# First LSTM steps as seven half-block products, two units in three sets, with the cell product on GpSimd

## The chip, the cores and the metric

The kernel runs on one core of one Trainium2 chip. The metric is device time in microseconds (us), the median of several runs. The engines are TensorE (PE: matmuls; PEld is its weight load), VectorE (DVE), ScalarE (ACT), GpSimd (POOL) and SyncE (SP, whose queue issues most DMAs). Matmul results land in PSUM, eight banks of 128 x 512 float32; everything else works from SBUF. Everything is float32.

## The reference, cut to what matters

Four layers are applied in turn to x [128 batches, 64 nodes, 256 features], each as x = x + layer(relu(layernorm(x))). The change touches the first one alone: two graph convolutions give h [128, 64, 256], and then four LSTMs, one for each window length p, run over windows of h and write each window's last hidden state back into it:

```python
def step(carry, x_t):
    h, c = carry
    g = x_t @ Wih.T + h @ Whh.T + bias
    i, f, gg, o = jnp.split(g, 4, axis=-1)
    c = sigmoid(f) * c + sigmoid(i) * tanh(gg)
    h = sigmoid(o) * tanh(c)
    return ((h, c), None)          # zero initial state
...
for p in range(1, MAX_SKIP + 1):   # MAX_SKIP = 4
    nw = Tv // p
    wins = h[:, :nw * p, :].reshape(Bv * nw, p, Hd)
    last = _lstm_last(Wih[p - 1], Whh[p - 1], bih[p - 1], bhh[p - 1], wins)
    idx = jnp.arange(nw) * p + (p - 1)
    h = h.at[:, idx, :].set(last.reshape(Bv, nw, Hd))
```

In a window's first step h and c are zero: the f gate plays no part, and the three gates i, g and o come from x alone (256 features in, 3 x 256 out). Later steps need four gates from x and h (512 in, 4 x 256 out).

## The kernel before, in words

h lies in four tiles `hs`, [128 features of a half c, c, node, 32 batches]. The LSTM works in units: one window length p, two of the tiles (two blocks of batches, `blk`), and nk windows (8, 8, 7, 8 for p = 1 to 4), so a block has n = nk x 32 columns, 256 or 224. The loop at L565 runs over p, then over pairs of units (8, 4, 3 and 2 pairs, 17 in all), then over the steps t, and in each step over the two units. `unit` (L429) makes a unit's closures and `step` (L519) issues one step.

A step with t = 0 uses `first_gates` (L452): for each gate and each half m of its outputs, a bank is filled by four matmuls (two halves c of the features, two blocks), 24 in a step and 48 for a pair, each of 128 x 128 weights by 128 x n columns (L459). ACT applies the gate function from PSUM (`act`, L444 to L446). DVE multiplies i by g into the cell (L529), ACT takes its tanh (L538), and DVE multiplies with o into the hidden state (L540), or, in the last step of a window, into `hs` (L547).

A later step uses `next_gates` (L466). It splits weights and moving data into 2 x 2 blocks, and computes each pair of gates by seven block products in place of eight (Winograd's form of Strassen's algorithm). `sums` (L190) makes four sums of weight blocks, once per p, in `blocks_of` (L551), which also negates one block (L561); `moving_blocks` (L497) makes four differences of the moving blocks in each step (L504 to L509). `sevens` (L208) pairs them up and `seven` (L153) issues them: products 1, 5, 6 and 7 into four banks, two copies out of PSUM on ACT (L162, L163), two additions on DVE (L165, L166); then, in `finish`, one addition on POOL (L169), products 2, 4 and 3 on top of three of the banks, two more DVE additions (L174, L177), and the gate functions through `end`. Each product is four matmuls here (two gates, two chunks, L471). `finish` is called at once.

Written order is a priority only. The tile framework fills each engine's queue by a plan of its own: an instruction is placed when its inputs and its tile's buffer are planned to be ready, the earliest written first. On the chip each engine then works its queue strictly in that order. The buffers that can hold an instruction back are eight PSUM banks, and for tags `gates` three, `p15`, `diff` and `state` two each, and five weight tiles `w` in pool `lw`. A sixth weight tile (`weight_tile`, L63) gets the attention weights (L572), whose DMA is issued at 16 us. In p = 4's last pair of units, four groups of residual work (`to_residual`, L225: a copy each on ACT and POOL, 16 transposes, two DVE additions) are written between the steps with t = 0 and 1 (L585).

## Time and profile before

| what | us |
|---|---|
| median of three runs (2576.1 to 2579.25) | 2576.28 |
| the profiled execution's own time | 2575.58 |
| its span, first to last instruction | 2573.6 |
| LSTM, from its first matmul to the first of the attention | 181 to 1269 |
| busy time of the first steps' matmuls (L459, 1632 records) | 346.2 |
| busy time of ACT's gate functions from PSUM (L446, 332) | 190.6 |

The granted TensorE clock has a mean of 0.995. Each float32 matmul leaves two records, so 1632 records are 816 matmuls. In a row of groups, the name of the line, the engine and the operation come first, then the tiles written and read, shape and count; after the bar the busy time in us and the mean of one record in ns; last the idle time of that engine just before, and what ended it. Matmul records overlap each other, so a record's mean (379 ns) is more than its share of the busy time. A row of stretches gives, after the stretch and its length, the busy time of PE, PEld, DVE, ACT and POOL, the granted clock, and the DMA's share and GB/s.

### The profile page before, as it was taken

Reading aid. Unit: us, or ns where it says so; the run is one execution under the profiler, and the core shown is the slowest. Engines: PE = TensorE matmul, PEld = TensorE weight load, DVE = VectorE, ACT = ScalarE, POOL = GpSimd, SP = SyncE. Lnnn points to the kernel's source line nnn. Section 1 sums busy time; section 2 is a strip of 40 time slices with the busy share of each in tenths; the row PEclk is TensorE's granted clock in tenths of the full one; section 3 lists DMA queues with packets and bytes.
Section 4 is the critical chain, followed back from the end, with each engine's and each line's share of the span. In section 5 each row is a group of like instructions: output and inputs, shape, how many; then the busy total and the mean of one; then the engine's idle time right before and its main releaser. Section 6 shows DMA issues by size and latency. Waiting matters only on the chain.

```text
span 2573.6 us, 46531 instructions
## 1 busy us (share of the span) xinstructions
PE 2521.9 (98%) x20388; PEld 2082.3 (81%) x20388; DVE 1290.4 (50%) x2317; ACT 1086.2 (42%) x1829; POOL 353.7 (14%) x299
## 2 busy tenths in 40 slices
PE   6999999999999999999999999998999999999998
PEld 4668888889999998888866664444889889889887
DVE  6632234445545555565566666423645545545544
ACT  3544444444444443344455456472333332332332
POOL 3420000000101001111123221003110110111110
PEclk9999999999999999999999999998999999999999
DMA  5100000001000000000200000001000000000000
GB/s 172 51 2 1 1 17 1 1 1 33 1 1 1 1 17 1 1 1 1 83 2 2 2 18 1 1 19 39 10 9 10 18 9 10 18 9 9 18 10 17
DMA packets 30203, 39.66 MB, mean 15 GB/s; under 512 B 1712, under 2 KB 26416, under 8 KB 30000
## 3 DMA queue, kind: packets, MB, share of 16 engines
q1 hardware_dynamic: 29136, 36.09, 4.2%
q8 instruction: 160, 2.62, 0.4%
q10 hardware_dynamic: 864, 0.59, 0.1%
q14 instruction: 43, 0.35, 0.0%
HBM read 28.29 MB, written 8.39 MB: 14 GB/s over the span
## 4 chain that ended last, share of the span: by engine, by line
PE 93%; DVE 4%; POOL 1%; ACT 1%; issue 1%; DMA 0%; DVEq 0%; POOLq 0%; SPq 0%; ACTq 0%
PE ps L471 28%; PE ps L972 15%; PE ps L459 13%; PE ps L1017 8%; PE ps L652 4%; PE ps L873 4%; PE ps L936 4%; PE ps L134 3%; PE ps L625 3%; PE ps L668 2%; PE ps L380 2%; PE ps L404 2%; DVE st L91 1%; POOL rstd L95 1%; PE ps L729 1%; PE ps L117 1%
## 5 line engine op out<-in xcount | busy, mean ns | idle before, releaser
L972 PE MATMUL ps<-arena 128*128 128x256 f32 x1792 | 391.8, 380 | 0.2 <-DVE arena L186 0.2
L972 PEld LDWEIGHTS ps<-arena 128*128 128x128 f32 x1792 | 338.0, 190 | 53.5 <-issue 7.5
L446 ACT ACTIVATE gates<-ps,lbias 128x512 f32<-128x512 f32 (+3 forms) x332 | 190.6, 594 | 413.1 <-PE ps L471 259.0
L459 PE MATMUL ps<-h,w 128*128 128x256 f32 (+1 forms) x1632 | 346.2, 374 | 0.0
L459 PEld LDWEIGHTS ps<-h,w 128*128 128x128 f32 x1632 | 309.8, 190 | 35.1 <-issue 0.5
L471 PE MATMUL ps<-diff,s 128*128 128x256 f32 (+1 forms) x1536 | 326.6, 369 | 0.0
L471 PEld LDWEIGHTS ps<-diff,s 128*128 128x128 f32 x1536 | 291.4, 190 | 24.8
L169 POOL TENSOR_TENSOR gates<-p 128x512 f32<-128x512 f32 (+1 forms) x64 | 82.9, 1296 | 971.4 <-DVE p L166 971.4
L446 ACT ACTIVATE gates<-gates,lbias 128x512 f32<-128x512 f32 (+3 forms) x256 | 139.5, 592 | 120.4 <-DVE gates L174 102.1
L204 ACT ACTIVATE arena<-arena 128x512 f32<-128x512 f32 x144 | 89.4, 630 | 181.6 <-POOL arena L169 103.0
L1017 PE MATMUL ps<-arena 128*128 128x128 f32 x1280 | 153.0, 276 | 1.4 <-DVE arena L192 1.0
L1017 PEld LDWEIGHTS ps<-arena 128*128 128x128 f32 x1280 | 147.0, 192 | 2.9 <-PE ps L1017 1.7
L169 POOL TENSOR_TENSOR arena<-arena 128x512 f32<-128x512 f32 x64 | 72.8, 1138 | 540.0 <-DVE arena L166 540.0
L625 PE MATMUL ps<-arena,w 128*128 128x512 f32 x256 | 116.6, 609 | 1.3 <-DVE arena L146 1.1
L471 PE MATMUL ps<-diff,w 128*128 128x256 f32 (+1 forms) x512 | 116.3, 370 | 0.7 <-DVE p L166 0.7
L174 DVE TENSOR_TENSOR arena<-arena,ps 128x512 f32<-128x512 f32 x64 | 39.8, 621 | 152.5 <-PE ps L972 84.2
L471 PE MATMUL ps<-h,w 128*128 128x256 f32 (+1 forms) x512 | 115.8, 369 | 0.0
L471 PE MATMUL ps<-state,w 128*128 128x256 f32 (+1 forms) x512 | 115.8, 369 | 0.0
L471 PE MATMUL ps<-state,s 128*128 128x256 f32 (+1 forms) x512 | 115.8, 369 | 0.0
L652 PE MATMUL ps<-hT,w 128*128 128x512 f32 x256 | 112.8, 593 | 0.0
L873 PE MATMUL ps<-arena,w 128*128 128x512 f32 x256 | 110.6, 593 | 0.7 <-ACT arena L866 0.7
L174 DVE TENSOR_TENSOR gates<-p,ps 128x512 f32<-128x512 f32 (+1 forms) x64 | 42.3, 661 | 128.8 <-PE ps L471 128.7
(177 smaller groups left out, 3769.8 us busy)
## 6 DMA issues: line engine op xcount, KB each, us to landing
x<-in_x SPq DMA_DIRECT2D x28, 512.0 KB, 5.0
out<-x SPq DMA_DIRECT2D x16, 512.0 KB, 3.0
w<-in_wih SPq DMA_DIRECT2D x4, 1024.0 KB, 9.0
w<-in_whh SPq DMA_DIRECT2D x3, 1024.0 KB, 4.8
arena<-in_l3w SPq DMA_DIRECT2D x3, 1024.0 KB, 5.0
w<-in_wqkv SPq DMA_DIRECT2D x1, 768.0 KB, 13.6
wg<-in_wg ACTq DMA_DIRECT2D x2, 256.0 KB, 3.9
w<-in_w1t SPq DMA_DIRECT2D x1, 512.0 KB, 3.8
```

Source lines behind the costliest of these rows:

```text
L169: nc.gpsimd.tensor_tensor(out=out[1][1], in0=p1, in1=p5, op=ALU.add)
L174: nc.vector.tensor_tensor(out[1][0], p1, ps[3], ALU.add)
L204: nc.scalar.activation(out[m][n], out[m][n], func)
L446: nc.scalar.activation(o, ps, func, bias=lbias[:, col : col + 1])
L459: nc.tensor.matmul(ps[:, blk, 0:n].rearrange("p (k b) -> p k b", b=HB), lhsT=wi[:, c, col : col + P], rhs=x_of(0, blk)[:, c], start=c == 0 ...
L471: nc.tensor.matmul(ps[:, r], lhsT=w[:, c, j, :], rhs=moving[c], start=first and r == 0 and c == 0, stop=c == 1, skip_group_check=True,)
L625: nc.tensor.matmul(ps, lhsT=w1[:, c, m * P : (m + 1) * P], rhs=a[:, 2 + c, :], start=(c == 0), stop=(c == 1),)
L652: nc.tensor.matmul(ps, lhsT=wqk[:, c, col : col + P], rhs=hT[:, c, :], start=(c == 0), stop=(c == 1),)
L873: nc.tensor.matmul(pss[m], lhsT=w2[:, c, m * P : (m + 1) * P], rhs=a[:, c, :], start=(c == 0), stop=(c == 3),)
L936: nc.tensor.matmul(ps[:, t, :], lhsT=w[:, t * P : (t + 1) * P], rhs=b, start=first and t == 0, stop=True, skip_group_check=True,)
L972: nc.tensor.matmul(ps[:, r, :], lhsT=w[:, c, col : col + P], rhs=b[:, c, :], start=first and r == 0 and c == 0, stop=c == 1, skip_group_ch ...
L1017: nc.tensor.matmul(ps[:, t, :], lhsT=w[:, c, t * P : (t + 1) * P], rhs=b[:, c, :], start=first and t == 0 and c == 0, stop=c == 3, skip_gr ...
```

## The change

The first steps now use the seven products too. For x alone the 2 x 2 blocks are: weights by feature half c and output half m, moving data by feature half c and batch block. A product is then two matmuls, one for each of two gates, and a set of two gates has 14. Two units need six gates, taken as three sets: i and g of the first unit, o of both units, i and g of the second unit (`first_steps`). `gate_set` replaces `first_gates` and `next_gates`; where both gates of a set have the same function and bias, one activation serves both.

`take` and `flush` put the sets behind each other: a set's first part (products 1, 5, 6, 7) is written first, then the second part of the set before it, and then what follows from that (cell, tanh, hidden state). With p = 1 this goes on from pair to pair; with p > 1 `flush` ends it before the later steps. The cell product i x g of a first step moves from DVE to POOL (`new_cell`).

`first_blocks` makes the sums of weight blocks for the first steps: for p = 1 into a tile of pool `lw`, later into the tile `weight_tile`, ahead of the next p. The sums for the later steps (`blocks_of`) are now written behind the first pair's first steps, and the attention weights' load behind the last pair's. The negated weight block is dropped: the fourth difference has its operands swapped instead. The residual work moves to the steps with t = 1 and 2.

```diff
-            def unit(p, tiles, k0, nk, wi, wh, ws):
...
+                return lambda t, blk: win[blk][:, :, :, t, :], cell, hid
+            def gate_tile():
+                return lp.tile([P, 2, 2, 2, 256], F32, tag="gates", name="gates", bufs=3)
+            def by_chunk(blocks):
+                return [[b[:, c] for c in range(2)] for b in blocks]
+            def gate_set(p, n, g, gates, w, bs):
+                pairs = [sevens(w, b, lambda *wb: wb) for b in bs]
+                def product(i):
+                    def issue(ps, first):
+                        for r, j, _ in gates:
+                            for c, (wc, bc) in enumerate(zip(*pairs[r][i])):
+                                nc.tensor.matmul(
+                                    ps[:, r], lhsT=wc[:, j, :], rhs=bc,
+                                    start=first and r == 0 and c == 0, stop=True,
+                                    skip_group_check=True,
+                                )
+                    return issue
+                out = [[g[:, :, m, blk, 0:n] for blk in range(2)] for m in range(2)]
+                p15 = lp.tile([P, 2, 2, 256], F32, tag="p15", name="p15")
+                same = gates[0][1:] == gates[1][1:]
...
+                def end(m, blk, ps):
+                    if m == 1 and blk == 1:
+                        return
+                    for r, j, func in gates[:1] if same else gates:
+                        r = slice(0, 2) if same else r
+                        o = g[:, r, m, blk, 0:n] if m == 0 else g[:, r, m, :, 0:n]
+                        act(o, o if ps is None else ps[:, r], j, m, func)
+                return seven(
+                    {i: product(i) for i in range(1, 8)}, [bank((P, 2, 256))[:, :, 0:n] for _ in range(4)],
+                    p15[:, 0, :, 0:n], p15[:, 1, :, 0:n], out, end,
+                )
-                    if t == 0:
-                        first_gates(pairs[0], ig)
-                        nc.vector.tensor_tensor(cell, gate_i, gate_g, ALU.mult)
-                        first_gates(pairs[1][1:], fo)
...
+            def output(t, p, u, gate_o, th):
+                x_of, cell, hid = u
+                nc.scalar.activation(th, cell, AF.Tanh)
+                if t < p - 1:
+                    nc.vector.tensor_tensor(hid, gate_o, th, ALU.mult)
+                else:
+                    for blk in range(2):
+                        o, h = (
+                            v[:, :, blk, :].rearrange("p c (k b) -> p c k b", b=HB) for v in (gate_o, th)
+                        )
+                        nc.vector.tensor_tensor(x_of(t, blk), o, h, ALU.mult)
+            behind = []
+            def take(start, then):
+                finish = start()
+                flush()
+                behind.append((finish, then))
+            def flush():
+                while behind:
+                    finish, then = behind.pop()
+                    finish()
+                    then()
+            def first_steps(p, n, two, w0):
+                bs = []
+                tt = dp.tile([P, 4, 2, 256], F32, tag="diff", name="diff")
+                for u, (x_of, _, _) in enumerate(two):
+                    ts = [tt[:, i, u, 0:n] for i in range(4)]
+                    x = [[x_of(0, blk)[:, c] for blk in range(2)] for c in range(2)]
+                    differences(
+                        nc.vector, *x[0], *x[1],
+                        *[d.rearrange("p (k b) -> p k b", b=HB) for d in ts], negate=True,
                     )
+                    bs.append(([[x[0][0]], None], [[x[1][0]], [x[1][1]]], [[d] for d in ts]))
+                igs = [gate_tile() for _ in range(2)]
+                both = gate_tile()
+                def new_cell(i):
+                    def then():
+                        gate_i, gate_g = (igs[i][:, r, :, :, 0:n] for r in range(2))
+                        nc.gpsimd.tensor_tensor(out=two[i][1], in0=gate_i, in1=gate_g, op=ALU.mult)
+                        if i == 1:
+                            out(1)
+                    return then
+                def out(i):
+                    output(0, p, two[i], both[:, i, :, :, 0:n], igs[i][:, 1, :, :, 0:n])
+                ig = [(0, 0, AF.Sigmoid), (1, 2, AF.Tanh)]
+                o = [(i, 3, AF.Sigmoid) for i in range(2)]
+                take(lambda: gate_set(p, n, igs[0], ig, w0, [bs[0]] * 2), new_cell(0))
+                take(lambda: gate_set(p, n, both, o, w0, bs), lambda: out(0))
+                take(lambda: gate_set(p, n, igs[1], ig, w0, [bs[1]] * 2), new_cell(1))
...
-                    nc.vector.tensor_tensor(ts[3], ts[1], h1, ALU.subtract)
+                nc.vector.tensor_tensor(ts[3], h1, ts[1], ALU.subtract)
+                b = (by_chunk([x1]) + [None], by_chunk([h1, h2]), by_chunk(ts))
+                ig, fo = gate_tile(), gate_tile()
...
+                gate_set(p, n, ig, [(0, 0, AF.Sigmoid), (1, 2, AF.Tanh)], ws, [b] * 2)()
+                nc.vector.tensor_tensor(gate_i, gate_i, gate_g, ALU.mult)
+                gate_set(p, n, fo, [(0, 1, AF.Sigmoid), (1, 3, AF.Sigmoid)], ws, [b] * 2)()
+                nc.vector.tensor_tensor(cell, cell, gate_f, ALU.mult)
+                nc.vector.tensor_tensor(cell, cell, gate_i, ALU.add)
+                output(t, p, u, gate_o, gate_g)
+            def first_blocks(wi, room):
+                wx = wi.rearrange("p c (j m f) -> p c m j f", m=2, f=P)
+                s0 = room.rearrange("p a (i j f) -> p (a i) j f", i=2, f=P)
+                ss = [s0[:, i] for i in range(4)]
+                a = [[wx[:, c, m] for c in range(2)] for m in range(2)]
+                sums(nc.vector, *a[0], *a[1], *ss)
+                return [[[b] for b in row] for row in a] + [[[b] for b in ss]]
...
-                nc.vector.tensor_scalar(wm[:, 1], wm[:, 1], -1.0, None, ALU.mult)
-                return (wx[:, 0], wm[:, 0]), (wx[:, 1], wm[:, 1]), ss
+                return [by_chunk([wx[:, m], wm[:, m]]) for m in range(2)] + [by_chunk(ss)]
+            w0 = first_blocks(w_next[0], lw.tile([P, 2, 1024], F32, tag="w", name="s"))
             for p, nk in ((1, 8), (2, 8), (3, 7), (4, 8)):
+                n = nk * HB
                 wi, wh = w_next
-                ws = blocks_of(wi, wh) if p > 1 else None
                 if p < 4:
                     w_next = (load_w(wih, p), load_w(whh, p))
-                else:
-                    w_att = weight_tile()
-                    nc.sync.dma_start(
-                        out=w_att[:, :, 0:768], in_=wqkv.rearrange("(c p) f -> p c f", p=P)
-                    )
-                    wqk, wv = w_att[:, :, 0:512], w_att[:, :, 512:768]
                 starts = range(0, NODES // p // nk * nk, nk)
                 units = [(tiles, k0) for tiles in ((0, 1), (2, 3)) for k0 in starts]
                 for j in range(0, len(units), 2):
-                    two = [unit(p, *u, nk, wi, wh, ws) for u in units[j : j + 2]]
-                    for t in range(p):
-                        for i, step in enumerate(two):
-                            step(t)
-                            if p == 4 and j == 2 and 2 * t + i < NK:
-                                to_residual(2 * t + i, xs[2 * t + i], back_pool, 1)
+                    two = [unit(p, *u, nk) for u in units[j : j + 2]]
+                    first_steps(p, n, two, w0)
+                    if p > 1:
+                        flush()
+                        if j == 0:
+                            ws = blocks_of(p, wi, wh)
+                    if j + 2 == len(units):
+                        if p < 4:
+                            w0 = first_blocks(w_next[0], weight_tile())
+                        else:
+                            w_att = weight_tile()
+                            nc.sync.dma_start(
+                                out=w_att[:, :, 0:768], in_=wqkv.rearrange("(c p) f -> p c f", p=P)
+                            )
+                            wqk, wv = w_att[:, :, 0:512], w_att[:, :, 512:768]
+                    for t in range(1, p):
+                        for i, u in enumerate(two):
+                            next_step(t, p, n, u, ws)
+                            if p == 4 and j == 2 and 2 * t + i - 2 < NK:
+                                to_residual(2 * t + i - 2, xs[2 * t + i - 2], back_pool, 1)
                             if p == 4 and j == 2 and t == p - 1 and i == 0:
                                 h = back_pool.tile([P, GT, D], F32, tag="hc", name="h")
```

## The prediction

> **What bounds the kernel now.** I read the page's engine shares first, then the chain that ended last, then the chain in the stretch the change rewrites, then the price rows. The page: TensorE (PE) is busy for 98% of the span and carries 93% of the chain. L459 (the first LSTM steps) is 13% of it, L471 (the later steps) 28%.
>
> ```profile
> span 2573.6 us, 46531 instructions
> PE 2521.9 (98%) x20388; PEld 2082.3 (81%) x20388; DVE 1290.4 (50%) x2317; ACT 1086.2 (42%) x1829; POOL 353.7 (14%) x299
> PE 93%; DVE 4%; POOL 1%; ACT 1%; issue 1%; DMA 0%; DVEq 0%; POOLq 0%; SPq 0%; ACTq 0%
> ```
>
> A busy PE is not a saturated one, so I asked for the chain from 181 to 360 us (the one-step windows), the engines' busy time there, and one hand-over between the two kinds of step:
>
> ```profile
> 180.71 0.86 PE ps L404 x2
> 181.56 178.49 PE ps L459 x827
> 181.00:354.00 173.00, 173.00 (x802) 152.12 (x801) 42.38 (x51) 86.27 (x118) 0.00 (x0) 1.00 0.02 7
> 899.96 32.80 PE ps L471 x173
> 932.76 20.72 PE ps L459 x96
> 953.48 6.69 PE ps L471 x31
> ```
>
> The chain is matmul behind matmul and nothing else, at granted clock 1.00. One pair of first steps takes 20.72 us for its 96 records, two to a matmul: 48 matmuls of 0.432 us. ACT is half busy (86.27 of 173), DVE a quarter (42.38), POOL not at all. So a matmul removed here shortens the program if the other engines stay ahead.
>
> The price rows, from the groups with shapes kept apart:
>
> ```profile
> L459 PE MATMUL ps<-h,w 128*128 128x256 f32 x1344 | 291.2, 379 | 0.0
> L459 PE MATMUL ps<-h,w 128*128 128x224 f32 x288 | 55.0, 352 | 0.0
> L162 ACT COPY p<-ps 128x512 f32<-128x512 f32 x40 | 23.4, 586 | 9.6 <-PE ps L471 6.6
> L166 DVE TENSOR_TENSOR p<-p,ps 128x512 f32<-128x512 f32 x40 | 27.5, 687 | 25.9 <-PE ps L471 25.9
> L529 DVE TENSOR_TENSOR state<-gates 128x1024 f32<-128x1024 f32 x28 | 34.3, 1225 | 119.8 <-ACT gates L446 119.8
> L192 DVE TENSOR_TENSOR arena<-arena 128x256 f32<-128x256 f32 x16 | 6.7, 419 | 0.0
> L192 POOL TENSOR_TENSOR arena<-arena 128x1024 f32<-128x1024 f32 x1 | 2.4, 2350 | 0.1
> ```
>
> Last, what happens when POOL and DVE both read SBUF (timeline at 985 us):
>
> ```profile
> 985.66 0.68 DVE L508 TENSOR_TENSOR diff<-state,diff 128x512 f32<-128x512 f32 x1
> 985.88 1.59 POOL L169 TENSOR_TENSOR gates<-p 128x512 f32<-128x512 f32 x1 [11.27 <-DVE p L166]
> 986.38 1.65 DVE L509 TENSOR_TENSOR diff<-diff,state 128x512 f32<-128x512 f32 x1
> ```
>
> The POOL add, 1.27 us by its median, took 1.59 behind a DVE operation already running; the next DVE operation, 0.69 alone, took 1.65 and ended 0.56 us after the POOL add. They take turns, for whole instructions. DVE operations with one input in PSUM (L174) keep 0.69 us beside POOL.
>
> **The change, part by part.**
>
> *Matmuls removed.* A pair of first steps goes from 48 matmuls to three sets of 7 products by 2, that is 42. There are 17 pairs (8, 4, 3 and 2 for the four window lengths). One eighth of L459's busy time goes: (291.2 + 55.0) / 8 = 43.3 us. That is the whole gain.
>
> *Work added per pair on the others, against 42 x 0.432 = 18.1 us of PE.*
> - ACT, an i/g set: two copies 1.17; two 256-wide activations from PSUM 0.84 (the later steps run this pair in that); two 512-wide 1.33; two 256-wide 0.91; sum 4.25, twice. The output-gate set: 1.17 + 0.69 + about 1.05 (1024 wide, as the tanh L538) + 0.69 = 3.6. Two tanh 2.1. Sum 14.2 us, 78% of 18.1.
> - DVE: 12 additions 8.2; eight 256-wide differences at 0.42, 3.4; the hidden states 2.5. Sum 14.1 us, 78%. The cell products (2 x 1.22) leave it.
> - POOL: three additions 3.8; two cell products at 2.35, 4.7. Sum 8.5 us.
>
> None exceeds 18.1, so in mean PE stays the bound; the cover is 4 us a pair on ACT and DVE, where it was about 10 and 15.
>
> *Cell product on POOL.* 2.35 us instead of 1.22, at this shape. Behind it wait the tanh and then the hidden state, which the next step of that unit needs a whole step later. The GPSIMD Engine Reference of the Trainium skill (Engine selection) speaks against the move: two-input elementwise work belongs on VectorE, GpSimd being about twice as slow. The rows bear its ratio out, 2.35 to 1.22; if every excess stood on the path, 34 x 1.13 = 38 us would go and the change would bring 5. No reader of the cell lies on PE's path, so I charge the excess at nothing.
>
> What I do charge is turns. A DVE operation with two SBUF inputs (differences, hidden states, weight sums) can be held up to 2.35 us, and the PSUM additions behind it with it.
>
> *Banks, while one-step windows run.* A set's first part (four products, 3.45 us) needs four of eight banks. The set before still holds up to four; the one before that has just issued its last product. Its two DVE additions end about 0.9 us after their products (0.2 us to start, as L177 at 380.17 us behind the matmul beginning at 379.97, plus 0.69). If the bank longest free is taken, the last one is needed 2.59 us in, a margin of 1.7. If banks go round in fixed order, the second product (0.86 us in) waits 0.05 or so, 51 x 0.05 = 2.6 us. A held DVE operation of 2.35 exceeds the margin by 0.65. PE then lags and the lag is cover for what follows, so most pairs should not pay twice. Between 0 and 14 us (8 pairs, two holds of 0.65, a fixed-order wait of 0.2): I take 4, nearer the low end since these stretches have no idle row today.
>
> *Hand-over to the next steps, 9 pairs.* From the end T of the output-gate set's products: addition, T+0.9; activation, T+1.7; hidden state 1.22, T+3.0; two additions of the last set, T+4.3; two differences, T+5.7. PE meanwhile runs the last set's second part (2.59) and two products of four matmuls (3.45) and wants the second difference at T+6.04. Slack 0.4 us, where today the first unit's hidden state is ready 9 us ahead (358.44 against 367.67). Between 0 and 2.35 (one hold) each, 0 to 21 us; I take 0.6 x 9 = 5.4, since the second cell product starts only after those differences when nothing is late.
>
> *Weight sums moved.* The four 1.22 us sums for the next steps come after the first steps, and their room is free only when the previous window length has ended. About 12 to 18 us remain at a DVE load of three quarters: 3 to 4.5 us free for 4.9 us of work. Between 0 and 4.9 for each of three lengths; I take 3 in all, most of it at length 2. The three negations (L561, 1.22) fall away, and the new sums for the first steps (4 x 0.69 per length) run under the PE-bound steps before: nothing, and without that cover 2.8 us each.
>
> *Moved with nothing charged.* The attention weights' load goes from 16 us to the last pair, SP's queue with it; 13.6 us to land, with over 100 us of steps ahead of its first use; behind it on SP are the x loads issued at 1263 us. Uncovered it would cost 13.6. The residual work of the last pairs moves by two steps, same instructions (16 transposes, two 1.2 us copies, two DVE additions for each of four groups) and the PE-bound later steps around it; its POOL copies already hold L540 (2.22 against 1.22). Uncovered, about 3 us a group.
>
> *Sum.* 43.3 - 4 - 5.4 - 3 = 30.9 us. The profiled execution took 2575.58 (span 2573.6 and 2.0 around it): 2544.7. The median of the three runs is 0.7 above the profiled one: 2545.4, so 2545.
>
> **The rivals.**
> 1. *All hidden.* The framework places each engine's instructions by readiness (today a difference for length 2 runs at 204 us, 150 us early), so waits may vanish: 2576.3 - 43.3 = 2533. For it: no idle row on L459 or L471 but 0.7 us. Against: 0.4 us of slack at the hand-over.
> 2. *Half given back.* Turns of POOL and DVE hit most pairs: 14 + 0.6 x 9 + 3 = 22 us lost gives 2555, and with a full hold at each hand-over (21 + 4 + 3 = 28) 2561. For it: L509 is held in most of the later steps today (mean 975 ns against 684 of its neighbour). Against: sums below 18.1.
> 3. *Slower: in-order queues make the DVE and ACT chain the bound.* If an early-placed tanh or hidden state waits on a POOL cell product with the next set's copies and additions queued behind it, PE waits for that chain in each pair: addition 0.9, activations 0.9, cell 2.35, tanh 1.05, copies 1.2 make 6.4 us where 3.45 us of products cover, so 3.0 us a pair and 17 x 3.0 = 51: 2576.3 - 43.3 + 51 = 2584. It decides from 43.3/17 = 2.55 us a pair. For it: ACT and DVE at 78%, one ACT queue carrying tanh and copies. Against: today's order puts a tanh ahead of an output-gate activation written before it (190.82 against 191.96 us), so order follows readiness.
> 4. *No effect on the matmul count* can't be: 42 are issued for 48.
>
> **How the numbers follow.** Forecast (2538 to 2551) 0.45; all hidden 0.17; half given back 0.20; slower 0.18, of which a third ends within 0.2%. A measurement of this kernel can tell about 0.2% (5 us) from no change. Faster 0.82, same 0.06, slower 0.12. Range: full gain with a little from the early weight sums that leave the opening stage, 2531; upwards through the second rival to the point where the third begins, 2574.
>
> **What would show it.** L459's 1632 matmul records gone, 1428 in their place; about 18.1 to 18.6 us per pair of one-step windows; PE idle by DVE in the first products of a set and where a difference is late; POOL products of 2.35 us and some DVE two-input operations over 1.6 us. Wrong if PE idles more than 2.5 us a pair, behind ACT copies that follow a tanh, or if the first steps' matmuls take more than 0.432 us.

## The result, and the profile after

The changed kernel takes 2577.41 us (median of 4 runs, 2576.97 to 2578.61), beside 2577.77 for the kernel before: a ratio of 0.9999, 95% interval 0.9982 to 1.0017. The forecast was 2545 us. There is no gain.

The page of the changed kernel, its span, engine shares and the shares of the chain that ended last:

```profile
span 2574.9 us, 46812 instructions
PE 2492.7 (97%) x20184; PEld 2045.8 (79%) x20184; DVE 1457.1 (57%) x2636; ACT 1132.3 (44%) x1982; POOL 506.7 (20%) x384
PE 80%; DVE 9%; ACT 5%; POOL 3%; issue 2%; DMA 1%; SPq 0%; DVEq 0%; POOLq 0%; ACTq 0%
```

The 204 matmul records are gone (20388 to 20184), which is 1632 less 1428, as the change says. PE is busy for 29 us less and the span is 1.3 us longer than it was: PE now waits. Its share of the chain falls from 93% to 80%, and DVE, ACT and POOL come in. The chain through the one-step windows, which was one run of matmuls in the kernel before, shows it (shares of the stretch from 186 to 343 us by line, then some of its pieces: start, length, what):

```profile
by line: PE ps L458 28.5%; ACT gates L472 13.5%; POOL state L534 12.4%; issue 11.6%; DVE gates L174 5.8%; DVE h L499 5.4%; ACT gates L491 5.4%; DVE diff L184 4.5%; DVE diff L188 2.9%; DVE diff L186 2.9%; DVE gates L177 2.3%; DVE p L166 2.3%
...
238.60 2.38 POOL state L534
242.69 3.73 PE ps L458 x16
...
258.25 2.38 POOL state L534
262.34 3.73 PE ps L458 x16
```

In the new numbering L458 is the matmul line of all LSTM steps, L472 the gate functions on ACT, L491 the tanh of the cell, L493 and L499 the hidden state on DVE, L534 the cell product on POOL, L184 to L188 the differences of a first step and L557 to L562 those of a later one. The pattern comes back every 19.65 us (242.69, 262.34, 281.99): that is a pair of one-step windows, forecast at 18.1 to 18.6.

Where the time stands, by the first LSTM matmul and the first attention matmul (us). Idle is PE's: the time from the start of one LSTM matmul record to the next beyond the usual spacing, which is 0.216 us (0.189 with 224 columns), summed where it exceeds 0.2 us; records at a reduced clock are left out. The brackets of the timelines count from the modelled end of a record, and so show some 0.16 us less for the same stretch.

| | LSTM starts | LSTM lasts | PE idle in it |
|---|---|---|---|
| before | 181.4 | 1088.3 | 1.0 |
| after | 186.2 | 1083.8 | 33.7 |

So two things ate the gain. The LSTM gave 4.5 us of the 43.3 that its matmuls gave up, and the stage ahead of it, which the forecast charged at nothing, became 4.8 us longer. The rest is within 1 us of before.

Most of the idle 33.7 us lies in two places. In the one-step windows each pair loses about 1.3 us, 8.6 us in all. This is the timeline of one (start, length, engine, line, operation, tiles, shapes; in brackets the idle time before it and what ended it):

```profile
238.60 2.37 POOL L534 TENSOR_TENSOR state<-gates 128x1024 f32<-128x1024 f32 x1 [1.43 <-ACT gates L472]
241.00 1.06 ACT L491 ACTIVATE gates<-state 128x1024 f32<-128x1024 f32 x1 [1.53 <-POOL state L534]
241.97 0.67 ACT L472 ACTIVATE gates<-ps,lbias 128x512 f32<-128x512 f32 x1
242.69 1.99 PE L458 MATMUL ps<-diff,s 128*128 128x256 f32 x8 [0.83 <-ACT gates L472]
```

The tanh stands in ACT's queue in front of a gate function that reads a PSUM bank. ACT stands still for 1.53 us until the cell arrives from POOL. Only then is the bank read, and PE waits for the bank. This stretch is 0.99 us long by the measure of the table; another 0.32 us a pair ends with a DVE addition (L174).

The other place is the hand-over to the later steps, nine times, 22.1 us in all over the stretches above 0.5 us. In seven of them PE waits for an addition, 12.6 us together. The first of these:

```profile
366.71 2.86 POOL L534 TENSOR_TENSOR state<-gates 128x1024 f32<-128x1024 f32 x1 [6.36 <-ACT gates L472]
...
369.60 1.06 ACT L491 ACTIVATE gates<-state 128x1024 f32<-128x1024 f32 x1 [2.07 <-POOL state L534]
...
370.69 1.22 DVE L493 TENSOR_TENSOR state<-gates 128x1024 f32<-128x1024 f32 x1 [3.33 <-ACT gates L491]
...
371.83 0.68 DVE L165 TENSOR_TENSOR p<-p,ps 128x512 f32<-128x512 f32 x1
...
373.03 0.68 DVE L166 TENSOR_TENSOR p<-p,ps 128x512 f32<-128x512 f32 x1
...
373.76 1.56 PE L458 MATMUL ps<-diff,w 128*128 128x256 f32 x6 [2.04 <-DVE p L166]
```

POOL's product, then the tanh, then the hidden state, which has stood at the head of DVE's queue for 3.33 us. Behind it in that queue are the two additions that read the next set's banks (L165, L166), and behind these PE. The second unit's hidden state is not wanted yet; it is only in front.

The other 9.5 us at the hand-overs are four waits for a difference of the first unit's next step (L561, 7.8 us) and two for a copy (L162, 1.7 us). Two of the four stand in the last pairs of lengths 2 and 3, where the weight sums for the next length's first steps come ahead of that difference in DVE's queue, and an operation is held while POOL makes a cell product. At length 2 it is a sum (L195), 2.84 us where its neighbours take 0.69:

```profile
575.09 2.84 DVE L195 TENSOR_TENSOR w<-w 128x512 f32<-128x512 f32 x1
577.86 0.68 DVE L561 TENSOR_TENSOR diff<-state,diff 128x512 f32<-128x512 f32 x1
578.68 0.67 PE L458 MATMUL ps<-diff,s 128*128 128x256 f32 x2 [1.77 <-DVE diff L561]
```

Two waits of the changed kernel sum this up (from 181 to 1270 us; engine, tile and line, what it waited for, the sum, how often, the longest):

```profile
ACT gates L491 <- POOL state L534: 57.0, 34, 2.1
DVE state L493 <- ACT gates L491: 33.1, 19, 3.3
```

All 34 tanh behind a first step's cell waited, 1.68 us in the mean.

### The profile page after: what moved, and what is told of

The parts are those of the page before. It is cut to its first block, busy times and chain, and to the rows that moved or that the text cites. A ratio compares the mean times of both kernels' runs of the same rounds, so it can differ in the third digit from the quotient of the medians.

```text
span 2574.9 us, 46812 instructions
## 1 busy us (share of the span) xinstructions
PE 2492.7 (97%) x20184; PEld 2045.8 (79%) x20184; DVE 1457.1 (57%) x2636; ACT 1132.3 (44%) x1982; POOL 506.7 (20%) x384
## 4 chain that ended last, share of the span: by engine, by line
PE 80%; DVE 9%; ACT 5%; POOL 3%; issue 2%; DMA 1%; SPq 0%; DVEq 0%; POOLq 0%; ACTq 0%
PE ps L458 29%; PE ps L1010 15%; PE ps L1055 8%; PE ps L690 4%; PE ps L911 4%; PE ps L974 4%; PE ps L134 3%; ACT gates L472 3%; PE ps L663 3%; POOL state L534 2%; PE ps L706 2%; PE ps L380 2%; PE ps L404 2%; ACT gates L491 1%; DVE state L493 1%
## 5 line engine op out<-in xcount | busy, mean ns | idle before, releaser
L458 PE MATMUL ps<-diff,s 128*128 128x256 f32 (+1 forms) x1824 | 397.2, 372 | 13.4 <-DVE diff L561 7.1
L458 PEld LDWEIGHTS ps<-diff,s 128*128 128x128 f32 x1824 | 344.8, 190 | 51.6 <-issue 8.9
L472 ACT ACTIVATE gates<-gates,lbias 128x512 f32<-128x512 f32 (+4 forms) x426 | 240.5, 619 | 192.1 <-DVE gates L174 166.5
L169 POOL TENSOR_TENSOR gates<-p 128x512 f32<-128x512 f32 (+1 forms) x115 | 154.1, 1340 | 734.0 <-DVE p L166 710.4
L458 PE MATMUL ps<-diff,w 128*128 128x256 f32 (+1 forms) x1040 | 242.0, 374 | 13.5 <-DVE p L166 12.3
L458 PE MATMUL ps<-h,w 128*128 128x256 f32 (+1 forms) x1028 | 241.0, 371 | 0.0
L458 PEld LDWEIGHTS ps<-diff,w 128*128 128x128 f32 x1040 | 196.4, 191 | 37.0 <-DVE p L166 16.4
L458 PEld LDWEIGHTS ps<-h,w 128*128 128x128 f32 x1028 | 194.8, 190 | 18.9 <-issue 0.5
L472 ACT ACTIVATE gates<-ps,lbias 128x256 f32<-128x256 f32 (+3 forms) x213 | 91.4, 476 | 238.3 <-PE ps L458 238.3
L174 DVE TENSOR_TENSOR gates<-p,ps 128x512 f32<-128x512 f32 (+1 forms) x115 | 76.5, 665 | 119.0 <-PE ps L458 118.6
L165 DVE TENSOR_TENSOR p<-p,ps 128x512 f32<-128x512 f32 (+1 forms) x115 | 76.3, 663 | 101.4 <-PE ps L458 77.1
L174 DVE TENSOR_TENSOR arena<-arena,ps 128x512 f32<-128x512 f32 x64 | 39.8, 621 | 152.2 <-PE ps L1010 84.2
L663 PE MATMUL ps<-arena,w 128*128 128x512 f32 x256 | 117.4, 613 | 1.4 <-DVE arena L146 1.3
L458 PE MATMUL ps<-state,s 128*128 128x256 f32 (+1 forms) x512 | 118.0, 374 | 0.0
L458 PE MATMUL ps<-state,w 128*128 128x256 f32 (+1 forms) x512 | 116.0, 370 | 1.4 <-ACT p L162 1.4
```

Of the source, the lines that this page charges most:

```text
L169: nc.gpsimd.tensor_tensor(out=out[1][1], in0=p1, in1=p5, op=ALU.add)
L174: nc.vector.tensor_tensor(out[1][0], p1, ps[3], ALU.add)
L458: nc.tensor.matmul(ps[:, r], lhsT=wc[:, j, :], rhs=bc, start=first and r == 0 and c == 0, stop=True, skip_group_check=True,)
L472: nc.scalar.activation(o, ps, func, bias=lbias[:, col : col + 1])
L663: nc.tensor.matmul(ps, lhsT=w1[:, c, m * P : (m + 1) * P], rhs=a[:, 2 + c, :], start=(c == 0), stop=(c == 1),)
```

## The experiments

Two theories at first. A: the loss in the LSTM comes from the cell product on POOL. B: it comes from the order of the sets, whose output gates stand between the two i/g sets. The opening's loss was put down to the weight sums for window length 1, which DVE has to make there.

All results, each beside the kernel before on the same chip. Its medians there were 2575.42 to 2577.26 us, so differences between two rows are good to some 2 us:

| kernel | median us | ratio, 95% interval | LSTM starts | LSTM lasts | PE idle in it |
|---|---|---|---|---|---|
| cell product on DVE | 2541.21 | 0.9856, 0.9842 to 0.9871 | 186.0 | 1049.2 | 4.5 |
| new method at length 1 alone | 2569.82 | 0.9971, 0.9962 to 0.9981 | 184.7 | 1077.3 | 9.6 |
| output gates last | 2598.71 | 1.0081, 1.0064 to 1.0098 | 185.4 | 1106.4 | 45.6 |
| output gates last, cell on DVE | 2557.08 | 0.9928, 0.9910 to 0.9946 | 184.7 | 1065.8 | 17.3 |
| weight sums later | 2567.59 | 0.9962, 0.9948 to 0.9977 | 176.5 | 1084.1 | 34.2 |
| cell on DVE, twice | 2556.15 | 0.9923, 0.9908 to 0.9938 | 186.4 | 1065.4 | 15.7 |
| cell on DVE, spare product on POOL | 2547.30 | 0.9889, 0.9874 to 0.9903 | 186.4 | 1057.3 | 11.7 |
| both tanh held back | 2570.75 | 0.9977, 0.9968 to 0.9986 | 184.2 | 1081.5 | 31.0 |
| and a hidden state held back | 2554.70 | 0.9917, 0.9899 to 0.9935 | 184.7 | 1063.8 | 17.1 |
| cell on DVE and weight sums later | 2530.76 | 0.9828, 0.9811 to 0.9844 | 176.7 | 1049.2 | 4.5 |

Every kernel with the new method idles for 0.7 us in its first set, where PE waits for the first differences; it is in the last column.

**The cell product back on DVE.**

```diff
-nc.gpsimd.tensor_tensor(out=two[i][1], in0=gate_i, in1=gate_g, op=ALU.mult)
+nc.vector.tensor_tensor(two[i][1], gate_i, gate_g, ALU.mult)
```

> The changed kernel with one part undone: the cell product of the first steps back on DVE. Theory A (the length of the cell product on POOL: tanh waits 2.4 to 2.9 us for it with the activations of the next set queued behind it on ACT): 1.13 us less for each product on the chain, two at each of 9 hand-overs and one in each of 8 pairs with p = 1, 29 us, so about 2548. Theory B (the order of the sets: whatever engine makes the cell, its chain ends too late for the next step): at most 10 us, about 2567 or more.

One line, and 36.2 us of the changed kernel's time go, more than theory A's 29. The LSTM lasts 1049.2 us, 39.1 less than before. The chain from 186 to 343 us of this kernel is matmuls again, 720 records in 155.64 us, so 18.16 a pair of 84:

```profile
187.43 0.14 issue
187.56 155.64 PE ps L458 x720
```

The busy times of PE, PEld, DVE, ACT and POOL over the stretch from 186 to 343 us, first of the changed kernel, then of this one:

```profile
186.00:343.00 157.00, 150.03 (x679) 127.60 (x678) 120.12 (x197) 104.51 (x182) 67.02 (x39) 1.00 0.00 1
```

```profile
186.00:343.00 157.00, 156.46 (x725) 137.46 (x724) 135.25 (x226) 111.93 (x195) 33.36 (x26) 1.00 0.02 8
```

DVE is busier here, 135.25 of 157 us or 86% against 77%, and past its first set PE does not idle. The relief that the product's move gave DVE bought nothing; what it did to the order of arrival cost 36 us. Nearly the whole of the LSTM's loss is theory A's. The 34.6 us between the two LSTM lengths (1083.8 and 1049.2) are 29.2 us of idle time (33.7 less 4.5), 3.0 us of a reduced clock (see the last section), and 2.4 us in stretches too short for the table.

**The new method at length 1 alone**, the old first steps at lengths 2 to 4.

```diff
-                    first_steps(p, n, two, w0)
+                    if p == 1:
+                        first_steps(p, n, two, w0)
+                    else:
+                        for u in two:
+                            first_plain(p, n, u, wi)
```

`first_plain` is `first_gates` of the kernel before with its cell product on DVE.

> One part alone: seven products for the first steps with p = 1 only, the old first steps for p = 2 to 4 (cell on DVE there, weight sums at the top of each p). If the waits lie mainly at the hand-overs to the later steps (22 us of PE gaps by the trace, against 22.6 us gained there), the hand-overs and their gain both go: 20.7 us gained with p = 1, less 9.7 us of gaps there and 4.8 us in the opening stage, about 2571. If the change's loss sat with p = 1 instead, 2577 or above.

The LSTM is 11.0 us shorter than before. Length 1 alone removes 8 x 2.55 = 20.4 us of matmuls, less the 8.6 us that PE idles between 188 and 352 us in the changed kernel: 11.8, which agrees. So in the changed kernel the nine pairs of lengths 2 to 4, which remove 22.9, made the LSTM 6.5 us longer: there, and mostly at the hand-overs, more was lost than the method gains.

**The output gates last**: i and g of both units first, then the output gates of both.

```diff
                         nc.gpsimd.tensor_tensor(out=two[i][1], in0=gate_i, in1=gate_g, op=ALU.mult)
-                        if i == 1:
-                            out(1)
...
-                take(lambda: gate_set(p, n, both, o, w0, bs), lambda: out(0))
                 take(lambda: gate_set(p, n, igs[1], ig, w0, [bs[1]] * 2), new_cell(1))
+                take(lambda: gate_set(p, n, both, o, w0, bs), outs)
```

> The changed kernel with the order of the three sets changed: i and g of the first unit, i and g of the second, then o of both; the cell product stays on POOL. Theory B (order): both cells and both tanh are ready before the last set ends, only an addition, an activation and a hidden state stand between it and the next step; gaps at a hand-over fall from 2.5 us to 1 us or less, 9 x 1.5 = 14 us, about 2562. Theory A (length on POOL): the products are as long as before and still stand before a tanh, less than 6 us, about 2572.

> The order of e3 (i and g of both units first, then the output gates of both) with the cell product on VectorE. If e3's 21 us against the changed kernel came from the order of the sets (both hidden states wait for the last set, and the later steps want the first one at once), the loss stays with the product on VectorE: 2541 + 15 to 22, so 2556 to 2563, with idle stretches of 2 us or more at the nine hand-overs. If it came from the product on GpSimd, it goes: 2541 to 2546.

This order is slower by 21.3 us than the changed kernel, where both theories had forecast less time than that, and with the product on DVE still slower by 15.9 than the first experiment. Theory B falls both ways: the set order of the change is the better one, with either engine. Why is seen where both hidden states come last (timeline of the kernel with output gates last and the cell on DVE, which has this diff and the one of the first experiment):

```profile
359.24 2.36 DVE L493 TENSOR_TENSOR state<-gates 128x1024 f32<-128x1024 f32 x2 [1.36 <-ACT gates L472]
359.50 0.58 ACT L163 COPY p<-ps 128x512 f32<-128x512 f32 x1
360.56 0.67 PE L458 MATMUL ps<-state,w 128*128 128x256 f32 x2 [1.92 <-ACT p L163]
```

The profile names the copy L163, but that ended at 360.08. The first of the two hidden states, half of the 2.36 us, ended at about 360.4, and the matmul that reads it starts at 360.56. In the order of the change a whole set lies between.

**The weight sums later.** The sums of weight blocks for length 1 are placed behind a copy of the opening's ninth group (`issue_after` puts what is issued under it behind a given instruction).

```diff
-            w0 = first_blocks(w_next[0], lw.tile([P, 2, 1024], F32, tag="w", name="s"))
+            with tc.issue_after(late):
+                w0 = first_blocks(w_next[0], lw.tile([P, 2, 1024], F32, tag="w", name="s"))
```

> The changed kernel with the sums of the weight blocks for p = 1 held back until the ninth group of the opening stage, so that DVE doesn't stand behind the weights' DMA at 16 us. Theory C (the first LSTM matmul comes 4.8 us later because of that wait, 2.3 us, and of a second stretch of 3.4 us at half the granted clock that follows it, 1.7 us): about 4 us less, 2573. If the opening loses them otherwise: 2577.

It gains 9.8 us where 4 were forecast, all ahead of the LSTM, which now starts at 176.5: the 4.8 us lost, and 4.9 more than the kernel before had. VectorE's queue near 16 us tells the first part. The changed kernel:

```profile
16.22 0.69 DVE L192 TENSOR_TENSOR s<-w 128x512 f32<-128x512 f32 x1 [2.44 <-DMA w<-in_wih]
16.83 0.68 DVE L194 TENSOR_TENSOR s<-w 128x512 f32<-128x512 f32 x1
17.54 1.29 DVE L146 COPY m<-ps 128x512 f32<-128x512 f32 x2
```

The same copy in the kernel before, and with the sums later:

```profile
15.23 1.29 DVE L146 COPY m<-ps 128x512 f32<-128x512 f32 x2
```

```profile
13.92 1.29 DVE L146 COPY m<-ps 128x512 f32<-128x512 f32 x2
```

A weight sum stands at the head of DVE's queue until its weights have landed, with the opening's own work behind it: 3.6 us of the 9.8. A second part is clock. The stretch around 55 us (length, then the five engines' busy time; the number after them is the granted clock) in the kernel before, in the changed one and with the sums later:

```profile
50.00:60.00 10.00, 8.47 (x131) 6.59 (x132) 7.48 (x21) 3.91 (x6) 5.10 (x5) 0.83 0.01 2
```

```profile
50.00:62.00 12.00, 7.52 (x79) 6.06 (x80) 7.74 (x19) 3.02 (x4) 5.83 (x5) 0.72 0.13 43
```

```profile
50.00:60.00 10.00, 10.00 (x156) 6.90 (x156) 4.96 (x14) 5.37 (x9) 3.98 (x3) 1.00 0.17 54
```

The idle stretches of PE there are followed by a reduced clock, which costs at most 12 x 0.28 = 3.4 us in the changed kernel, 1.7 before, and nothing here, where PE is not idle. With 3.6 that makes 7.0 of 9.8. Most of the rest are waits of PE for POOL (L389): 1.33 and 2.02 us long in the changed kernel, up to 51.32 and 53.80 us, and 0.27 and 0.99 for the same matmuls here. That this kernel is ahead of the kernel before by 1.3 us already at the copy goes back to a load: DVE's statistics wait for x until 11.76 us before, 10.45 here and 10.33 in the changed kernel. Why that load lands earlier stays open.

**What about the product on POOL costs?** A1: its length, because a reader is on PE's path. A2: its turns with DVE, which holds differences and sums. A3: the place that its readers have in the queues of ACT and DVE, in front of work that was ready.

For A1 the cell is made twice on DVE, 2.45 us, longer than 1.22 by about the excess of POOL, with no work on POOL:

```diff
+                        nc.vector.tensor_tensor(two[i][1], gate_i, gate_g, ALU.mult)
                         nc.vector.tensor_tensor(two[i][1], gate_i, gate_g, ALU.mult)
```

> Cell product on DVE, made twice in a row (2.45 us in place of 1.22), so that the chain through the cell is as long as with POOL's 2.35 us, by an engine whose durations the planner may know better and without POOL. Theory A1 (length): 2565 to 2577. Theories A2 (turns) and A3 (place): 2541 to 2548, the rest being DVE's own 42 us of extra work, which has 4 us of room in each pair.

14.9 us more than with one product, which lies between the two forecasts. The trace shows 11.2 us more idle time and 3.4 us of a reduced clock. It isn't the price of length alone, since DVE also does 42 us more work here. For A2 the cell stays on DVE, and POOL makes a product of the cell with itself that nobody reads:

```diff
                         nc.vector.tensor_tensor(two[i][1], gate_i, gate_g, ALU.mult)
...
+                        nc.gpsimd.tensor_tensor(out=spare, in0=two[i][1], in1=two[i][1], op=ALU.mult)
```

> Cell product on DVE as in e1_cell_dve, and beside it a product of the same size on POOL (cell times cell into a spare tile) that nothing reads. It leaves what POOL's product does to DVE by taking turns at SBUF, and takes away that anything waits for it. Theory A1 (length: the chain is 1.13 us longer on POOL) and theory A3 (place: the planner puts the tanh into ACT's queue as if POOL's product were short, and ACT then stands, 1.68 us on average, with ready activations behind it): as e1_cell_dve, 2541 to 2546. Theory A2 (turns: POOL's product holds DVE's two-input operations): back to 2560 to 2577.

6.1 us more, close to the forecast without turns (2546 at most) and far from the other (2560 or more). The spare product took 1.974 us in the mean at 256 columns where the real one took 2.509, and it starts later, behind the product on DVE; so 6 need not be what the real one's turns cost. The turns themselves are plain in the changed kernel; this difference takes 0.41 us alone:

```profile
229.93 2.48 POOL L534 TENSOR_TENSOR state<-gates 128x1024 f32<-128x1024 f32 x1 [1.95 <-DVE diff L184]
230.12 2.57 DVE L185 TENSOR_TENSOR diff<-h 128x256 f32<-128x256 f32 x1
```

The Trainium skill calls this an exclusive lock on a shared pair of SBUF ports, held for a whole instruction, between GpSimd and a DVE operation with two SBUF inputs (SBUF — State Buffer, "SBUF: two separate sides"). The row agrees: the DVE operation ends at 232.69, 0.28 us after the POOL product.

For A3 the product stays on POOL and only places are changed. First both tanh: the first unit's behind the output gates' last gate function, the second unit's behind the copies of the next set.

```diff
-                nc.scalar.activation(th, cell, AF.Tanh)
+                with tc.issue_after(after) if after else nullcontext():
+                    nc.scalar.activation(th, cell, AF.Tanh)
...
-                            out(1)
+                            deferred.append(lambda after: out(1, after))
```

> The changed kernel, cell product on POOL, but each tanh of a first step is held in ACT's queue behind work that comes before the product's real end: the first unit's behind the last activation of the output gates, the second unit's behind the copies of the next set. Theory A3 (place): most of the 36 us of e1_cell_dve come back, about 2545. Theory A1 (length): the tanh comes no earlier, 2570 or more. Theory A2 (turns): POOL's product is still there, 2570 or more.

6.7 us come back, but in the trace (of the slowest of ten runs, 2573.7 us) the LSTM is only 2.3 us shorter. By its own forecasts (2545 for the place, 2570 or more without it) this run speaks against A3. Its trace shows why so little came: at the hand-overs the second unit's hidden state still waits at the head of DVE's queue, and PE's idle time there is 17.5 us where it was 22.1. Timeline of this kernel (L494 is its tanh, L496 its hidden state, L167 and L168 the additions):

```profile
368.12 1.23 DVE L496 TENSOR_TENSOR state<-gates 128x1024 f32<-128x1024 f32 x1 [3.33 <-ACT gates L494]
...
369.26 0.68 DVE L167 TENSOR_TENSOR p<-p,ps 128x512 f32<-128x512 f32 x1
...
370.46 0.68 DVE L168 TENSOR_TENSOR p<-p,ps 128x512 f32<-128x512 f32 x1
...
371.20 2.63 PE L460 MATMUL ps<-diff,w 128*128 128x256 f32 x8 [2.00 <-DVE p L168]
```

The hidden state still stands 3.33 us in front of the two additions. So the last step puts the second unit's hidden state behind them:

```diff
+        mark["add"] = nc.vector.tensor_tensor(p5, p5, ps[3], ALU.add).ins
...
+                with tc.issue_after(add) if add else nullcontext():
+                    if t < p - 1:
+                        nc.vector.tensor_tensor(hid, gate_o, th, ALU.mult)
...
```

> As x2 (cell product on GpSimd, both tanh placed later), and the second unit's hidden state is placed on VectorE behind the next set's two additions out of PSUM. In x2 that hidden state stood 3.33 us at the head of VectorE's queue at 368.12 us with the additions behind it, and TensorE's idle stretches over 1.5 us at the nine hand-overs to the later steps sum to 17.5 us. If the place of the waiting instruction in VectorE's queue is what is left of the loss, these nine go: 2570.75 - 15 to 17.5, so 2553 to 2556. If the length of the product on GpSimd itself is what TensorE waits for (the chain product, tanh, hidden state), nothing is gained by the place: 2568 to 2574, and the idle stretches stay at about 2 us each.

2554.7 us, as the theory of the place has it; 16.05 us come from where one instruction of each pair stands in one queue. The same stretch (L497 is the hidden state):

```profile
364.87 2.64 POOL L543 TENSOR_TENSOR state<-gates 128x1024 f32<-128x1024 f32 x1 [4.92 <-ACT gates L474]
...
366.79 0.69 DVE L167 TENSOR_TENSOR p<-p,ps 128x512 f32<-128x512 f32 x1 [1.49 <-PE ps L460]
367.54 1.06 ACT L494 ACTIVATE gates<-state 128x1024 f32<-128x1024 f32 x1 [2.33 <-POOL state L543]
368.51 0.69 DVE L168 TENSOR_TENSOR p<-p,ps 128x512 f32<-128x512 f32 x1 [1.04 <-PE ps L460]
369.12 1.22 DVE L497 TENSOR_TENSOR state<-gates 128x1024 f32<-128x1024 f32 x1
```

POOL's product is as long as before, the tanh waits for it as long as before, and it costs nothing here: the additions now wait for PE and not PE for them. In seven of the nine hand-overs PE has no idle stretch above 0.5 us any more. The two that are left, 2.2 and 2.0 us, are the last pairs of lengths 2 and 3, with the weight sums and a held operation ahead of the difference that PE wants.

So of the 36.2 us that the product on POOL costs, 22.7 are its readers' places in the queues of ACT and DVE (2577.41 less 2554.70); by the traces the LSTM is 20.0 us shorter (1083.8 less 1063.8), most of it at the hand-overs, whose idle time falls from 22.1 to 4.2 us. The other 13.5 (to 2541.21) are in this kernel mostly PE's idle time, 12.6 us more than with the product on DVE, 8.5 of it in the one-step windows. There the new places gained nothing (8.6 before them): PE now waits for DVE, whose difference (L187) takes 2.57 us beside POOL's product, with the additions (L167, L176) behind it:

```profile
229.57 2.57 DVE L187 TENSOR_TENSOR diff<-h 128x256 f32<-128x256 f32 x1
233.13 1.99 PE L460 MATMUL ps<-diff,s 128*128 128x256 f32 x8 [0.27 <-DVE p L167]
235.87 1.13 PE L460 MATMUL ps<-diff,s 128*128 128x256 f32 x4 [0.74 <-DVE gates L176]
```

In these windows the unread product on POOL left no idle time and the doubled product on DVE 6.3 us, but there DVE has more work too. How the 13.5 part into turns and length isn't settled; the two single prices, 6.1 and 14.9, were taken with the queues as they fell out in those kernels, and needn't add up with the places.

**Both repairs**: the cell product on DVE and the weight sums later.

> Both repairs: cell product on DVE, and the sums of the weight blocks for p = 1 held back in the opening stage. If the two losses are independent, 2541 less 9.7 us, about 2531, which is the full 43 us of the matmuls and 3 us more. If the opening's gain is lost again where PE then waits, 2541.

2530.76 us, the fastest kernel of the study, at 0.9828 of the time before (0.9811 to 0.9844). The two losses add up: 36.2 + 9.8 = 46.0 from the single repairs, 46.65 measured. Its page:

```profile
span 2528.7 us, 46852 instructions
PE 2478.3 (98%) x20184; PEld 2044.5 (81%) x20184; DVE 1476.4 (58%) x2670; ACT 1134.0 (45%) x1982; POOL 422.3 (17%) x350
PE 91%; DVE 6%; POOL 1%; ACT 1%; issue 1%; DMA 1%; DVEq 0%; ACTq 0%; POOLq 0%
```

It issues the same 20184 matmul records as the changed kernel, in 46 us less.

## Why the prediction was wrong

**The gain was right.** 42 matmuls for 48, 43.3 us: in the best kernel the LSTM is 39.1 us shorter with 3.5 us more of idle time, so 42.6 of the 43.3 are accounted for.

**The step that failed** is "No reader of the cell lies on PE's path, so I charge the excess at nothing." It looked at who needs the cell's data and not at who stands behind its readers. The tanh and the hidden state are not urgent, but in a queue that is worked in order they make urgent work wait: a gate function that frees a bank, two additions that PE needs. Charged at nothing, it cost 36.2 us. The sentences beside it, which name the GPSIMD Engine Reference (Engine selection), had 38 us if every excess stood on the path, from the rows of 2.35 and 1.22 us. That this is near 36.2 is luck: 22.7 us went with the product as long as before.

**The third rival was the mechanism, and was dismissed on a weak row.** It named an early tanh or hidden state that waits for POOL with the next set's copies and additions behind it, which is what the two timelines show. Its size was 3.0 us a pair; measured are 34.6 / 17 = 2.0, and not the same in each pair. The argument against it was that today's order puts a tanh ahead of an output-gate activation written before it, "so order follows readiness". That same row was evidence for the rival: it shows that a tanh may be put in front. It was harmless there because its cell came from DVE in time.

**Hand-over to the next steps**: 5.4 charged, 22.1 measured. The 0.4 us of slack was worked out for the first unit's chain, and nearly holds with the product on DVE, where no single stretch at a hand-over exceeds 0.8 us. What overran it most, with 12.6 us, was the second unit's hidden state in DVE's queue; the sum had that unit's cell product start "only after those differences when nothing is late" and left its readers out. The first unit's own differences came late four times, for 7.8 us. A small slip in the comparison: 358.44 us is where today's hidden state starts; it is ready 8.0 us ahead, not 9.

**Banks in one-step windows**: 4 charged, 8.6 of idle time measured (the charge's upper bound of 14 is more than its terms, 8 x 1.5 = 12). The place was right, and the product on POOL is the cause: with it on DVE the idle time past the first set is 0. By which way isn't settled. In the changed kernel most of it ends with ACT, reading a bank late behind the tanh, which the charge didn't have; with the tanh moved, as much is left behind a held DVE operation, which it had.

**Turns of POOL and DVE**: carried by the second rival's 14 us and partly by the terms above; a product on POOL that nobody reads cost about 6, and what the real one's turns cost stays open.

**Weight sums for the later steps**: 3 charged; with the product on DVE all idle time in the LSTM past the first set is 3.8 us, and no stretch of it is longer than 0.73. Whatever part of it is due to these sums, the term was not larger than charged by more than 0.8.

**The opening** is the second failed step: the new sums "run under the PE-bound steps before: nothing". At length 1 there are no such steps before. The sums lie in the opening, where DVE is on the path, and wait there for a DMA: 4.8 us lost, 9.8 to be had by placing them later. At lengths 3 and 4 the sums weren't free either: they come at the hand-over of the last pair before, where PE idles for 0.9 and 1.2 us even with the product on DVE.

**The moved load of the attention weights and the moved residual work** were charged at nothing, and the time from the first attention matmul to the end agrees: 1303.9 us before, 1302.8 in the best kernel.

## What to carry to other kernels

When an operation moves to a slower engine, don't ask only who needs its result: list what stands behind each of its readers on the readers' engines, because a reader that waits at the head of an in-order queue blocks work that is ready, and in this kernel that was most of the cost (22.7 of 36.2 us). A busy share says little about it: DVE at 86% let PE run without a gap, DVE at 77% with late inputs didn't. An operation that waits for a DMA may be better placed near where its result is wanted than where its engine first has room; here that brought 9.8 us.

## What the runs showed of the hardware

A TensorE idle stretch of only about 2 us can be followed by some 3 us at a reduced granted clock. The changed kernel, two of its hand-overs and then the one at 366 us (granted clock behind the five engines' busy times):

```profile
511.00:517.00 6.00, 5.81 (x19) 4.84 (x20) 3.43 (x5) 1.33 (x2) 1.64 (x1) 0.72 0.00 0
1127.00:1133.00 6.00, 6.00 (x22) 4.92 (x22) 2.43 (x4) 2.32 (x5) 0.42 (x1) 0.74 0.01 3
```

```profile
366.30:369.70 3.40, 3.40 (x16) 3.02 (x17) 1.05 (x2) 1.33 (x4) 2.86 (x1) 1.00 0.00 0
```

The idle stretches ahead of all three are 2.13 to 2.14 us long by the measure of the table. After two the clock fell, at a cost of 6 x 0.28 + 6 x 0.26 = 3.2 us, which is twice 3.2 us at half clock (the stretch from 55.87 to 59.27 us shows 0.50); after the third it didn't. In the kernel with the output gates last, with idle stretches of 2.4 to 4.6 us, it fell after six of nine. The Trainium skill has an activity window of about 3.4 us that runs freely and lets the clock fall after an idle one (TensorE: Matmul & The Clock Gate, "What's actually happening"), and advises against idle gaps above about 3 us ("Why this matters for your kernels"). The length of the slow stretches agrees. The bound on the gap does not: 2.1 us were enough here, sometimes. Why the clock fell after some stretches of this length and not after others, no run here shows.
